# Four stacked layers on one core: the steps of the windowed attention put into another order on every engine

## The chip, the cores and the metric

The kernel runs on one core of a Trainium2 chip. The metric is device time in microseconds (us) for one execution of the whole kernel; a median of several runs is given. A core has five engines that each work through their own instructions in order and wait for one another by semaphores: TensorE (PE, matmuls and transposes, results into PSUM), VectorE (DVE), ScalarE (ACT), GpSimd (POOL) and SyncE (SP), which here only issues DMAs.

## The reference: what is computed

The input has 8 images of 128 channels and 56 x 56 pixels. Four layers follow one another, each as x = x + layer(group norm(x)): a windowed attention (layer 0), a recurrent network over the pixels (layer 1), a partly masked 3x3 convolution (layer 2) and a residual pair of 3x3 convolutions (layer 3). The change touches layer 0 alone, which is in the main:

```python
proj = xw @ W_qkv + b_qkv                   # 49 windows of 8x8 pixels per image
logit = einsum('npc,nqc->npq', q_win * SCALE, k_win)     # window means
r_idx = top_k(logit, 4)                                  # 4 windows for each window
k_sel, v_sel = kv of those 4 windows                     # 256 keys
attn = softmax(einsum('bmqc,bmkc->bmqk', q_h * SCALE, k_sel))   # 8 heads of 16 channels
o = einsum('bmqk,bmkc->bmqc', attn, v_sel)
out = (o + depthwise3x3(v_img)) @ W_o + b_o
```

## The kernel before, in words

All is in fp32. Layer 0 has 8 x 49 = 392 windows, worked off as 196 pairs. One loop iteration p (L739 to L803) does the softmax of pair p+1 and finishes pair p. Its steps are:

- `scores(p+1)` (L492, matmul L504): 8 matmuls for the two windows of the pair, into four PSUM banks `s0` to `s3`, one buffer each. Bank g holds heads of group g for both windows, so a bank is free for the next pair when both exponentials that read it are done.
- `maxima` (L510, L512, DVE): one reduction per bank, four in all. `exponentials` (L514, L517, ACT): eight per pair, one per window and bank, each needs the maximum of its bank.
- `turn(W)` (L534, L540, PE): eight transposes of a window's exponentials into the PSUM tiles `pt0` and `pt1` (one buffer each), then two copies to SBUF, `pt0` by DVE (L542) and `pt1` by ACT (L543). The first window E of pair p+1 is turned at the end of iteration p, the second window O of pair p in the middle of iteration p.
- `divisors` (L522): a reciprocal on DVE (`rden`, L525) and two products on POOL (`rc`, L528); `turn_divisors` (L545, L549): two transposes on PE into the tile `po`.
- `values(p)` (L551, L559): 16 matmuls into `po`; they need both windows' copies and the fetched values `vs`. `spread` (L564, ACT) and `divide` (L568, DVE) read `po`.
- `gather` (L467, POOL) copies the chosen keys for pair p+2 (8 copies, 2 products). `fetch` (L482, SP) issues 8 DMAs per pair for the chosen values, with 6 window buffers.
- small pieces, one matmul group and one evacuation each, all through one PSUM bank `pp` (pool `ps_p`): queries (L380, evacuated L384 on DVE), keys (L283, L292 DVE), value image (L296, L302 ACT), value pixels (L314, L326 DVE), projection (L436, L441 DVE, and a `bn_stats` L449 that is put into `tails`), depthwise convolution (24 matmuls L410, evacuated L417 on ACT).
- "light" pieces of the next images: mean (L211, then 4 tiny DVE operations), variance (L224, 3 tiny DVE operations, then a Newton iteration of 12 tiny operations on POOL, L246 to L249), window means (L339) and routing (L350, then 4 tiny DVE operations).

The order on PE, ACT, DVE and POOL is written out by hand (`tc.manual_schedule`, L621): each engine runs its instructions in the order in which the loop body issues them. A planner (L697 to L714) decides ahead which small pieces go into which pair: `one` and `two` are two small pieces, or `two` is a depthwise convolution and there is usually no `one`; a `light` piece may come on top. In this text a **short pair** has two small pieces and a **long pair** has a depthwise convolution. In the loop of the kernel before, the piece `one` is issued ahead of `turn(O)`, its evacuation behind the copies of O, and the light piece at the very end behind `divide`. Before the loop there is a preamble for image 0 (L630 to L655); in it the PSUM tiles of the pieces go round the six banks of the scores and `pt`, and after it (`begun`) they all go to `pp`.

In the order of the issue in the old loop, a short pair is:

```python
PE :  scores  one  turn(O)  turn_divisors  values  two  turn(E)  light
DVE:  max0 max1  copy0(O)  end of one  max2 max3  hooks  end of two  tails  rden  copy0(E)  divide  light
ACT:  exp00 exp01  copy1(O)  exp10 exp11 exp02 exp03 exp12 exp13  spread  end of two (image)  copy1(E)
```

(expOG is window O, bank G; "hooks" are normalisations L270 with sums L275, and statistics L205, of later images.)

Of the kernel before, what the change touches and what calls it, by code (L numbers as in the profile page):

```python
# [44 lines left out]
def conv_stack_kernel(ctx: ExitStack, tc: tile.TileContext, a: dict, out: bass.AP):  # L45
# [80 lines left out]
    with ExitStack() as l0:  # L126
# [57 lines left out]

        def psum(shape, name):

            pool, tag = (ps_p, "pp") if begun else next(banks)
            return pool.tile(shape, F32, name=name, tag=tag)

        def store(wait, engine, dst, src):  # L190
# [320 lines left out]
            s_ = pairs[p]  # L511
            nc.vector.tensor_reduce(s_["nmax"][:, g, :], s_["s"][g], AX.X, ALU.max, negate=True)  # L512

        def exponentials(p, o, gs):  # L514
            s_ = pairs[p]
            for g in gs:
                nc.scalar.activation(  # L517
                    wins[2 * p + o]["e"][:, g, :], s_["s"][g][:, o, :], AF.Exp, bias=s_["nmax"][:, g, o : o + 1],
                    accum_out=s_["den"][:, o, g : g + 1],
                )  # L520

        def divisors(p):  # L522

# [10 lines left out]
        def turn(W):  # L534

            s_ = wins[W]
            pt = [ps_t.tile([P, 4, P], F32, name=f"pt_{W}_{c}", tag=f"pt{c}") for c in range(2)]
            for c in range(2):
                for g in range(4):
                    nc.tensor.transpose(pt[c][:, g, :], s_["e"][:, g, c * P : (c + 1) * P], ident)  # L540
            s_["eT"] = [win.tile([P, 4, P], F32, name=f"eT_{W}_{c}", tag=f"eT{c}") for c in range(2)]
            nc.vector.tensor_copy(s_["eT"][0], pt[0])  # L542
            nc.scalar.copy(s_["eT"][1], pt[1])  # L543

        def turn_divisors(p):  # L545

            po = pairs[p]["po"] = ps_o.tile([P, 2, 2, 2 * WPX], F32, name=f"po_{p}", tag="po")
            for o in range(2):
                nc.tensor.transpose(po[:, o, 1], pairs[p]["r"][:, o].rearrange("p g c -> p (g c)"), ident)  # L549

        def values(p):  # L551

            po = pairs[p]["po"]
            for o in range(2):
                s_ = wins[2 * p + o]
                for c in (1, 0):
                    for g in range(4):
                        ch = slice(g * CL, (g + 1) * CL)
                        nc.tensor.matmul(  # L559
                            po[ch, o, 0], s_["vw"][:, c, ch], s_["eT"][c][:, g, :],  # L560
                            start=(c == 1), stop=(c == 0),
                        )
# [25 lines left out]
        def run(f):  # L588
            for part in f[:2]:
                part()  # L590

# [50 lines left out]
        for i in (1, 3, 5):  # L642
            normalise(i, True)
        for f, i in ((normalise, 0), (normalise, 2), (sums, 0), (sums, 1), (normalise, 4), (sums, 2), (sums, 3),
                     (normalise, 6), (sums, 4), (sums, 5), (sums, 6)):
            f(i)
        for i in range(NBLK):
            run(keys[i])
# [1 line left out]
        pixels[0][0]()  # L650
        run(route)
        pixels[0][1]()
        for f in (queries(0, 0), image[0], image[1], *pixels[1:-1]):
            run(f)
        nc.scalar.activation(root, eps, AF.Exp)  # L655
        begun.append(True)
        job(-1, -1, lambda: pixels[-1])
        hook(-1, lambda: tails.extend(lambda f=f: run(f) for f in (queries(0, 1), image[2], image[3])))
        for i in range(4, NBLK):
            job(-1, min(pair_of(0, (i - 2) * NW) + 1, 2 * i), lambda i=i: image[i], True)  # L660
        hook(-1, lambda: neighbours(0, 0))

# [6 lines left out]
                job(last + 2, last + 5, lambda b=b, i=i: project(b, i))  # L669
        for b in range(1, B):  # L670

            at = [FIRST + (i > 2) for i in range(NBLK)] if b == 1 else [pair_of(b - 2, 0) + i for i in range(NBLK)]
            if b > 1:
                for i in range(NBLK):
                    hook(max(at[i] - 8, FIRST + i // 2), lambda b=b, i=i: load_x(b, i, i + 1, nc.gpsimd))
            for i in range(NBLK):
# [23 lines left out]
        for p in range(FIRST, END + 6):  # L700
            ready = [t for t in jobs if t[1] <= p and all(placed.get(k, p) < p for k in t[7])]
            light, long = (next((t for t in ready if t[5] == k), None) for k in (LIGHT, LONG))
            ready = [t for t in ready if t[5] == ONE]
            one = next((t for t in ready if not t[4]), None)
            if long:
                one, two = one if len(ready) > MANY else None, long
            else:
                two = next((t for t in ready if t is not one), None)
            plan[p] = (one, two, light)
            for t in filter(None, plan[p]):  # L710
                assert p <= t[0], ("late", p, t)
                jobs.remove(t)
                placed[t[6]] = p
# [25 lines left out]
        for p in range(FIRST, END + 6):  # L739
            now, then = 0 <= p < END, 0 <= p + 1 < END  # L740
            long = plan[p][1] and plan[p][1][5]
            one, two, light = (t and t[3]() for t in plan[p])
            E, O = 2 * p + 2, 2 * p + 1
            if then:
                scores(p + 1)
            if p + 2 < END:
                gather(E + 2)
                gather(E + 3)
                if p > FIRST + 1:
                    fetch(E + 2)  # L750
                    fetch(E + 3)
            for f in later:
                f()
            later.clear()
            for W in (2 * p - 2, 2 * p - 1):
                b, w = divmod(W, NWIN)
                if 0 <= b < B and w % NW == NW - 1:
                    join(b, w // NW)
            if then:
                maxima(p + 1, 0)  # L760
                maxima(p + 1, 1)
                exponentials(p + 1, 0, (0, 1))
            if one:
                one[0]()
            if now:
                turn(O)
                turn_divisors(p)
            if one:
                one[1]()
            if then:  # L770
                maxima(p + 1, 2)
                maxima(p + 1, 3)
                exponentials(p + 1, 1, (0, 1))
                exponentials(p + 1, 0, (2, 3))
                exponentials(p + 1, 1, (2, 3))
            early = two and (not one or long == LONG)
            if early:
                two[0]()
            if now:
                values(p)  # L780
                spread(p)
            if p == END - 1:
                nc.scalar.activation(root, eps, AF.Sqrt)
            if two and not early:
                two[0]()
            for f in hooks.get(p, ()):
                f()
            if two:
                two[1]()
            for f in tails:  # L790
                f()
            tails.clear()
            if then:
                divisors(p + 1)
                turn(E)
            if now:
                divide(p)
            if light:
                light[0]()
                light[1]()  # L800
            if p == FIRST + 1:
                for W in range(4):
                    fetch(W)  # L803
        for f in later:
            f()
        later.clear()
# [816 lines left out]
```

## Time and profile before

| what | value |
|---|---|
| median of 3 runs (lowest to highest) | 3633.07 us (3633.0 to 3638.25) |
| the profiled execution | 3636.9 us, its span 3635.1 us |
| layer 0 in the profile | about 0 to 1365 us |
| first and last score block (pair 0, pair 195) start | 27.71 us, 1358.17 us |
| layer 0, 0 to 1365 us: busy PE, DVE, ACT, POOL | 1306.96, 1098.33, 1093.96, 921.78 us |
| the other layers, 1365 to 3635.1 us: busy PE | 2241.41 of 2270.10 us |
| mean granted TensorE clock | 0.993 |

How to read it: an engine's busy time is the union of its instructions' times. PE's is modelled, so PE at 96% says that something was always in its pipeline, not that it ran at its rate. What paces layer 0 is therefore read from the start of one pair's score block to the start of the next, called a pair's period here. The starts of the score matmuls (L504) give 195 periods with a mean of 6.82 us and a median of 6.61 us. From pair 50 to pair 148 (four images) 98 periods take 666.8 us: 58 short pairs without a light piece take 6.58 us each (6.39 to 7.17), 24 long pairs without one 6.97 us (6.61 to 7.59), 8 short pairs with a light piece behind a DVE-evacuated piece 6.65 us, 4 short pairs with a light piece behind an image piece 8.32 us, and 4 long pairs with a light piece 7.86 us.

### The profile page before, as it was taken

How to read it: one execution, taken by the hardware profiler on the slowest of the kernel's cores; microseconds unless marked ns; L12 is line 12 of the kernel's file. 1: busy time of each engine (PE TensorE's matmuls, PEld its weight loads, DVE VectorE, ACT ScalarE, POOL GpSimd, SP SyncE). 2: the span in 40 equal slices, each digit the busy share in tenths (PEclk: the TensorE clock that was granted, in tenths of full speed). 3: DMA queues.
4: the chain of work that ended last, by engine and by line, in shares of the span. 5: the costliest groups of instructions: out<-in, count | busy, mean ns of one | idle time of the engine just before them, and what ended most of it. 6: DMA issues, size and time to landing. Idle time of an engine off the chain costs nothing.

```text
span 3635.1 us, 88662 instructions
## 1 busy us (share of the span) xinstructions
PE 3548.4 (98%) x31368; PEld 2936.7 (81%) x31368; DVE 1878.2 (52%) x3949; ACT 1673.0 (46%) x5263; POOL 1368.3 (38%) x3734
## 2 busy tenths in 40 slices
PE   8999999999999999999999999999999999999998
PEld 5666666666666668999999999999999833899998
DVE  6888888888888773222111111111122356757665
ACT  5787888888888883222222222222211245122222
POOL 4767677776666661111111111111000156323221
PEclk8999999999999999999999999999999999999999
DMA  5444444444444431111000000000022266000000
GB/s 146 120 121 115 111 123 112 124 113 122 108 107 111 121 91 56 47 44 47 1 1 1 1 1 1 1 1 1 7 57 59 55 171 170 21 21 26 29 21 35
DMA packets 201122, 238.25 MB, mean 66 GB/s; under 512 B 43120, under 2 KB 157680, under 8 KB 200672
## 3 DMA queue, kind: packets, MB, share of 16 engines
q0 software_dynamic: 34624, 117.03, 12.2%
q1 hardware_dynamic: 165216, 115.12, 11.4%
q8 instruction: 254, 4.16, 0.5%
q14 instruction: 196, 1.61, 0.2%
q10 hardware_dynamic: 832, 0.33, 0.0%
HBM read 133.80 MB, written 67.56 MB: 55 GB/s over the span
## 4 chain that ended last, share of the span: by engine, by line
PE 86%; DVE 6%; ACT 5%; issue 3%; POOL 0%; DMA 0%; SPq 0%; POOLq 0%; DVEq 0%; ACTq 0%
PE ps L950 32%; PE pt L540 8%; PE pc3b L1327 7%; PE pc3a L1327 7%; PE s L504 5%; PE po L985 5%; PE po L559 4%; PE pc L1173 4%; PE plep L410 3%; ACT e L517 3%; PE pi L925 2%; DVE nmax L512 2%; PE pc L1181 1%; PE pq L380 1%; PE pk L283 1%
## 5 line engine op out<-in xcount | busy, mean ns | idle before, releaser
L950 PE MATMUL ps<-hs,w_gates 128*128 128x136 f32 x7680 | 932.9, 280 | 0.4 <-DVE gk L962 0.4
L950 PEld LDWEIGHTS ps<-hs,w_gates 128*128 128x128 f32 x7680 | 911.1, 190 | 8.6 <-issue 0.6
L517 ACT ACTIVATE e<-s,nmax 128x256 f32<-128x256 f32 x1568 | 730.9, 479 | 245.2 <-DVE nmax L512 241.4
L973 ACT ACTIVATE hs<-ps,bg 128x136 f32<-128x136 f32 x744 | 237.3, 370 | 933.6 <-PE ps L950 926.1
L928 DVE SCALAR_TENSOR_TENSOR inp<-pi,bine,th 128x272 f32<-128x272 f32 x186 | 84.8, 497 | 888.7 <-ACT th L927 888.7
L512 DVE TENSOR_REDUCE nmax<-s 128x2 f32<-128x512 f32 x784 | 501.9, 682 | 22.5 <-PE s L504 22.3
L540 PEld LDWEIGHTS pt<-ident,e 128*128 128x128 f32 x3136 | 354.3, 141 | 187.0 <-issue 104.3
L540 PE MATMUL pt<-ident,e 128*128 128x128 f32 x3136 | 449.6, 279 | 26.1 <-ACT e L517 7.5
L914 POOL TENSOR_TENSOR xn<-X,ctr 128x136 f32<-128x136 f32 (+1 forms) x186 | 96.3, 537 | 874.9 <-PE pi L925 871.1
L950 PEld LDWEIGHTS ps<-inp,w_gates 128*128 128x128 f32 x2976 | 370.2, 190 | 13.5 <-PE pi L925 1.1
L950 PE MATMUL ps<-inp,w_gates 128*128 128x136 f32 x2976 | 375.3, 279 | 0.7 <-DVE inp L928 0.7
L517 ACT ACTIVATION_READ_ACCUMULATOR e<-s,nmax 128x1 f32 x1568 | 323.3, 206 | 0.0
L474 POOL COPY ks<-kT 128x64 f32 x1568 | 298.2, 234 | 48.3 <-ACT vrow L302 23.6
L528 POOL TENSOR_TENSOR rc<-rden,own 128x128 f32<-128x128 f32 x392 | 147.7, 396 | 372.1 <-DVE rden L525 236.2
L542 DVE COPY eT<-pt 128x512 f32<-128x512 f32 x392 | 263.6, 672 | 24.7 <-PE pt L540 16.8
L1327 PE MATMUL pc3b<-vb,u_w2c_t 128*128 128x224 f32 x1344 | 257.6, 353 | 0.0
L1327 PE MATMUL pc3a<-va,u_w1c_t 128*128 128x224 f32 x1344 | 255.6, 353 | 1.5 <-DVE va L1317 1.5
L1327 PEld LDWEIGHTS pc3a<-va,u_w1c_t 128*128 128x128 f32 x1344 | 254.2, 190 | 1.5 <-POOL va L1316 1.5
L1327 PEld LDWEIGHTS pc3b<-vb,u_w2c_t 128*128 128x128 f32 x1344 | 253.6, 190 | 0.0
L504 PE MATMUL s<-ks,qm 32*128 32x256 f32 x3136 | 250.1, 402 | 0.2
L543 ACT COPY eT<-pt 128x512 f32<-128x512 f32 x392 | 235.6, 601 | 5.4 <-PE pt L540 4.1
L559 PE MATMUL po<-eT,vs 128*32 128x128 f32 x6272 | 226.6, 277 | 10.6 <-ACT eT L543 10.5
(232 smaller groups left out, 4472.2 us busy)
## 6 DMA issues: line engine op xcount, KB each, us to landing
vs<-vpix SPq DMA_DIRECT2D x1568, 32.0 KB
v<-vimg POOLq DMA_DIRECT2D x56, 290.0 KB, 4.0
v<-vimg POOLq DMA_DIRECT2D x56, 289.5 KB, 4.9
v<-vimg POOLq DMA_DIRECT2D x56, 289.0 KB, 5.8
kept<-gk SPq DMA_DIRECT2D x56, 272.0 KB
g<-kept SPq DMA_DIRECT2D x56, 272.0 KB
xkeep<-X POOLq DMA_DIRECT2D x56, 224.0 KB, 2.4
out_dram<-y SPq DMA_DIRECT2D x56, 224.0 KB
```

The source lines that it names most:

```text
L474: nc.gpsimd.tensor_copy(kw[:, t : t + 1, :], ks[b][:, bass.ds(at, 1), :])
L504: nc.tensor.matmul(s_["s"][g][:, o, :], w["qm"][h].rearrange("p h x -> p (h x)"), w["kw"][h], start=True, stop=True,)
L512: nc.vector.tensor_reduce(s_["nmax"][:, g, :], s_["s"][g], AX.X, ALU.max, negate=True)
L517: nc.scalar.activation(wins[2 * p + o]["e"][:, g, :], s_["s"][g][:, o, :], AF.Exp, bias=s_["nmax"][:, g, o : o + 1], accum_out=s_["den"][: ...
L540: nc.tensor.transpose(pt[c][:, g, :], s_["e"][:, g, c * P : (c + 1) * P], ident)
L542: nc.vector.tensor_copy(s_["eT"][0], pt[0])
L543: nc.scalar.copy(s_["eT"][1], pt[1])
L559: nc.tensor.matmul(po[ch, o, 0], s_["vw"][:, c, ch], s_["eT"][c][:, g, :], start=(c == 1), stop=(c == 0),)
L950: nc.tensor.matmul(ps[f][:, i], w, src, start=(i == 0 and k == 0 and h != fresh), stop=(k == KH - 1 if h else k == KI - 1 and (s < WARM or ...
L973: nc.scalar.activation(hs[f][:, s % 2, i], ps[f][:, i], AF.Tanh, bias=bg[:, m : m + 1])
L985: nc.tensor.matmul(po, wout[:, k, :], hs[k // 2][:, :, k % 2], start=(k == 0), stop=(k == KH - 1))
L1327: nc.tensor.matmul(m[k], u[:, dy, k, :], v[:, k, i * WS + dy : i * WS + dy + WS, :], start=(dy == 0), stop=(dy == 2),)
```

## The change

The loop body becomes two written-out orders of named steps, one for long pairs (and for pairs with a scalar piece alone) and one for the rest. The second window is turned right behind the scores; in short pairs the piece `one` stands between that and `turn_divisors`/`values`, and its evacuation `end1` goes behind the third maximum. In long pairs all four maxima run before copy 0 of the second window, the first window's exponentials run first, and `turn_divisors` goes behind `values`. In both, ACT copies the turned first window (`new1`) ahead of the evacuation `end2`; DVE copies it (`new0`) ahead of `tails`, and `light`, `divisors` and `divide` come last, in this order. So on POOL a variance's Newton iteration now stands ahead of `rc`.

The planner no longer puts a light piece into a pair whose `two` is evacuated by ACT, unless it is due. The statistics of image 1 go into the preamble, except three; the seventh pixels piece goes into the preamble too; value-image block 2 uses the bank of `po` for once, and block 3 becomes a planned piece.

```diff
-            pool, tag = (ps_p, "pp") if begun else next(banks)
+            pool, tag = begun[-1] if begun else next(banks)
...
-            nc.vector.tensor_copy(s_["eT"][0], pt[0])
-            nc.scalar.copy(s_["eT"][1], pt[1])
+        def turned(W, c):
+            s_ = wins[W]
+            (nc.scalar.copy if c else nc.vector.tensor_copy)(s_["eT"][c], s_["pt"][c])
...
         for f, i in ((normalise, 0), (normalise, 2), (sums, 0), (sums, 1), (normalise, 4), (sums, 2), (sums, 3),
-                     (normalise, 6), (sums, 4), (sums, 5), (sums, 6)):
+                     (normalise, 6), (sums, 4), (sums, 5), (sums, 6), (once(measure, 1)[0], 0),
+                     (once(measure, 1)[0], 1)):
...
-        for f in (queries(0, 0), image[0], image[1], *pixels[1:-1]):
+        run(queries(0, 0))
+        for i in range(2, 4):
+            once(measure, 1)[0](i)
+        for f in (image[0], image[1], *pixels[1:]):
             run(f)
         nc.scalar.activation(root, eps, AF.Exp)
-        begun.append(True)
-        job(-1, -1, lambda: pixels[-1])
-        hook(-1, lambda: tails.extend(lambda f=f: run(f) for f in (queries(0, 1), image[2], image[3])))
-        for i in range(4, NBLK):
+        begun.append((ps_p, "pp"))
+
+        def second():
+
+            run(queries(0, 1))
+            begun.append((ps_o, "po"))
+            image[2][0]()
+            begun.pop()
+            image[2][1]()
+
+        hook(-1, lambda: tails.append(second))
+        for i in range(3, NBLK):
...
+            if light and two and two[4] and p < light[0]:
+                light = None
...
-            if then:
-                maxima(p + 1, 0)
-                maxima(p + 1, 1)
-                exponentials(p + 1, 0, (0, 1))
-            if one:
-                one[0]()
-            if now:
-                turn(O)
-                turn_divisors(p)
-            if one:
-                one[1]()
...
-            if then:
-                divisors(p + 1)
-                turn(E)
-            if now:
-                divide(p)
-            if light:
-                light[0]()
-                light[1]()
...
+        SHORT = """scores gather turn1 max0 max1 one turned old0 max2 exp00 exp01 old1 exp10 values end1 exp11 max3
+            two exp02 exp03 exp12 exp13 hooks turn0 spread new1 end2 new0 tails light divisors divide"""
+        LONGER = """scores gather turn1 max0 max1 exp00 old1 one end1 max2 max3 exp01 two old0 values turned exp02
+            exp03 exp10 exp11 exp12 exp13 hooks turn0 spread new1 end2 new0 tails light divisors divide"""
...
+            for name in (LONGER if plan[p][1] and (not plan[p][0] or plan[p][1][5] == LONG) else SHORT).split():
+                if name in acts:
+                    acts[name]()
```

In these strings `turn1`, `old0` and `old1` are the transposes and the two copies of the second window O, `turn0`, `new0` and `new1` those of the first window E; `turned` is `turn_divisors`, `end1` and `end2` are the evacuations of `one` and `two`. `gather` holds the gathers, the fetches, the stores put off from earlier pairs and the joins, as before.

More of the change, by code (lines that the diff above doesn't have):

```diff
@@ L512, in maxima, with exponentials @@
             nc.vector.tensor_reduce(s_["nmax"][:, g, :], s_["s"][g], AX.X, ALU.max, negate=True)
-        def exponentials(p, o, gs):
+        def exponentials(p, o, g):
             s_ = pairs[p]
[L516 to L520, printed above, removed]
+            nc.scalar.activation(
+                wins[2 * p + o]["e"][:, g, :], s_["s"][g][:, o, :], AF.Exp, bias=s_["nmax"][:, g, o : o + 1],
+                accum_out=s_["den"][:, o, g : g + 1],
+            )
         def divisors(p):
@@ L536, in turn, with outcome @@
             s_ = wins[W]
-            pt = [ps_t.tile([P, 4, P], F32, name=f"pt_{W}_{c}", tag=f"pt{c}") for c in range(2)]
+            s_["pt"] = [ps_t.tile([P, 4, P], F32, name=f"pt_{W}_{c}", tag=f"pt{c}") for c in range(2)]
             for c in range(2):
                 for g in range(4):
-                    nc.tensor.transpose(pt[c][:, g, :], s_["e"][:, g, c * P : (c + 1) * P], ident)
+                    nc.tensor.transpose(s_["pt"][c][:, g, :], s_["e"][:, g, c * P : (c + 1) * P], ident)
             s_["eT"] = [win.tile([P, 4, P], F32, name=f"eT_{W}_{c}", tag=f"eT{c}") for c in range(2)]
-            nc.vector.tensor_copy(s_["eT"][0], pt[0])
-            nc.scalar.copy(s_["eT"][1], pt[1])
+        def turned(W, c):
+            s_ = wins[W]
+            (nc.scalar.copy if c else nc.vector.tensor_copy)(s_["eT"][c], s_["pt"][c])
+        def outcome(p):
+            if "po" not in pairs[p]:
+                pairs[p]["po"] = ps_o.tile([P, 2, 2, 2 * WPX], F32, name=f"po_{p}", tag="po")
+            return pairs[p]["po"]
         def turn_divisors(p):
-            po = pairs[p]["po"] = ps_o.tile([P, 2, 2, 2 * WPX], F32, name=f"po_{p}", tag="po")
+            po = outcome(p)
             for o in range(2):
@@ L551, in values @@
         def values(p):
-            po = pairs[p]["po"]
+            po = outcome(p)
             for o in range(2):
@@ L670, in conv_stack_kernel @@
         for b in range(1, B):
-            at = [FIRST + (i > 2) for i in range(NBLK)] if b == 1 else [pair_of(b - 2, 0) + i for i in range(NBLK)]
+            at = [FIRST + 1] * NBLK if b == 1 else [pair_of(b - 2, 0) + i for i in range(NBLK)]
             if b > 1:
@@ L675, in conv_stack_kernel @@
                     hook(max(at[i] - 8, FIRST + i // 2), lambda b=b, i=i: load_x(b, i, i + 1, nc.gpsimd))
-            for i in range(NBLK):
+            for i in range(4 * (b == 1), NBLK):
                 hook(at[i], lambda b=b, i=i: once(measure, b)[0](i))
@@ L737, in conv_stack_kernel, with ahead @@
             cut += n
[L739 to L743, printed above, removed]
-            if then:
-                scores(p + 1)
-            if p + 2 < END:
[L747 to L751, printed above, removed]
+        SHORT = """scores gather turn1 max0 max1 one turned old0 max2 exp00 exp01 old1 exp10 values end1 exp11 max3
+            two exp02 exp03 exp12 exp13 hooks turn0 spread new1 end2 new0 tails light divisors divide"""
+        LONGER = """scores gather turn1 max0 max1 exp00 old1 one end1 max2 max3 exp01 two old0 values turned exp02
+            exp03 exp10 exp11 exp12 exp13 hooks turn0 spread new1 end2 new0 tails light divisors divide"""
+        def ahead(p):
+            if p + 2 < END:
+                for W in (2 * p + 4, 2 * p + 5):
+                    gather(W)
+                for W in (2 * p + 4, 2 * p + 5) if p > FIRST + 1 else ():
+                    fetch(W)
             for f in later:
@@ L758, in conv_stack_kernel @@
                     join(b, w // NW)
-            if then:
-                maxima(p + 1, 0)
-                maxima(p + 1, 1)
-                exponentials(p + 1, 0, (0, 1))
-            if one:
-                one[0]()
-            if now:
-                turn(O)
-                turn_divisors(p)
-            if one:
-                one[1]()
[L770 to L775, printed above, removed]
@@ L776, in conv_stack_kernel, with every, rest, root_table @@
-            early = two and (not one or long == LONG)
-            if early:
-                two[0]()
-            if now:
-                values(p)
-                spread(p)
+        def every(fs):
+            for f in fs:
+                f()
+        def rest():
+            every(tails)
+            tails.clear()
+        def root_table(p):
             if p == END - 1:
                 nc.scalar.activation(root, eps, AF.Sqrt)
-            if two and not early:
-                two[0]()
@@ L786, in conv_stack_kernel @@
-            for f in hooks.get(p, ()):
-                f()
-            if two:
[L789 to L793, printed above, removed]
-                divisors(p + 1)
-                turn(E)
-            if now:
-                divide(p)
-            if light:
-                light[0]()
-                light[1]()
-            if p == FIRST + 1:
-                for W in range(4):
-                    fetch(W)
+        for p in range(FIRST, END + 6):
+            now, then = 0 <= p < END, 0 <= p + 1 < END
+            one, two, light = (t and t[3]() for t in plan[p])
+            E, O = 2 * p + 2, 2 * p + 1
+            acts = {
+                "gather": lambda: ahead(p), "hooks": lambda: every(hooks.get(p, ())), "tails": rest,
+            }
+            if then:
+                acts.update(scores=lambda: scores(p + 1), divisors=lambda: divisors(p + 1), turn0=lambda: turn(E),
+                            new0=lambda: turned(E, 0), new1=lambda: turned(E, 1))
+                for g in range(4):
+                    acts[f"max{g}"] = lambda g=g: maxima(p + 1, g)
+                    for o in range(2):
+                        acts[f"exp{o}{g}"] = lambda o=o, g=g: exponentials(p + 1, o, g)
+            if now:
+                acts.update(turn1=lambda: turn(O), old0=lambda: turned(O, 0), old1=lambda: turned(O, 1),
+                            turned=lambda: turn_divisors(p), values=lambda: values(p), divide=lambda: divide(p),
+                            spread=lambda: (spread(p), root_table(p)))
+            if one:
+                acts.update(one=one[0], end1=one[1])
+            if two:
+                acts.update(two=two[0], end2=two[1])
+            if light:
+                acts["light"] = lambda: run(light)
+            for name in (LONGER if plan[p][1] and (not plan[p][0] or plan[p][1][5] == LONG) else SHORT).split():
+                if name in acts:
+                    acts[name]()
+            for W in range(4) if p == FIRST + 1 else ():
+                fetch(W)
```

## The prediction

> **What bounds the kernel now.** I read busy time by stretches first, then the chain of work that ended last, then each engine's timeline over one short pair. Layer 0 repeats almost exactly from image to image, so one pair says much.
>
> Busy time over 200 to 1200 us (columns: length, then PE, PE weight load, DVE, ACT, POOL, granted clock, DMA share, GB/s):
>
> ```profile
> 200.00:1200.00 1000.00, 968.61 (x11445) 657.91 (x11443) 827.50 (x1617) 817.82 (x2885) 698.33 (x2201) 1.00 0.45 114
> ```
>
> No engine but PE is full, and PE's number is modelled. The chain over two short pairs (start, length, what):
>
> ```profile
> 618.28 0.23 PE pt L540 x2
> 618.52 0.18 ACT e L517
> 618.70 0.04 issue
> 618.75 0.77 PE pt L540 x5
> 619.51 1.27 PE s L504 x16
> ...
> 624.06 0.95 PE pk L283 x2
> 625.01 0.23 PE pt L540 x2
> 625.25 0.19 ACT e L517
> ```
>
> PE is in it nearly always, but at each pair's end turn(E) stops for an exponential: PE is early there, and the softmax is what is late. DVE shows why:
>
> ```profile
> 620.71 1.28 DVE L512 TENSOR_REDUCE nmax<-s 128x2 f32<-128x512 f32 x2
> 622.34 0.69 DVE L542 COPY eT<-pt 128x512 f32<-128x512 f32 x1 [0.35 <-PE pt L540]
> 622.95 0.68 DVE L326 TENSOR_TENSOR vp<-pvp,bv_row 128x512 f32<-128x512 f32 x1
> 623.55 1.28 DVE L512 TENSOR_REDUCE nmax<-s 128x2 f32<-128x512 f32 x2
> ```
>
> Its copy of window O waits 0.35 us, because PE runs the piece `one` (1.00 us here) before turn(O); then the end of `one` stands ahead of the third maximum. ACT starts exp03 at 624.86, as the fourth maximum ends (624.83).
>
> So a short pair's loop is: max0 at t; exp03 at t+4.15 (620.71 to 624.86); 0.48 to its end (625.34); 0.84 from there through five transposes to the next scores (626.18); 1.27 from those to max0 (619.44 to 620.71; 1.17 where the scores don't wait). Sum 6.74 us, which is this period (619.44 to 626.18).
>
> **PE's own floor**, from starts of successive groups when nothing waits: scores 1.08, transposes 0.87 twice, `po` L549 0.31, values 1.10, pieces 0.86 (pixels 1.00): 5.95 us for a short pair. With a depthwise convolution (2.28) in place of two pieces 6.4; the trace has 6.61, and 6.80 when the scores wait 0.19 for the last exponential. Long pairs are PE's, short pairs the softmax's.
>
> **The change, part by part.**
>
> *turn(O) behind the scores; max2 ahead of end1 (short pairs).* No instruction is added. DVE issues these operations 0.60 us apart: max0 t, max1 t+0.60, copy t+1.21 (its transposes are then 0.5 us old, so the 0.35 wait goes), max2 t+1.81, end1 t+2.41, max3 t+3.01, done t+3.69. On ACT, from rows of pair 613 and this one: exp00 t+0.79, exp01 t+1.32, copy t+1.84, exp10 t+2.32, then 0.46 each: exp03 t+3.70. Maximum and ACT meet; I take t+3.73. The loop is 3.73+0.47+0.84+1.27 = 6.31, or 6.2 after a long pair. What is late next: everything nearly at once. PE's `two` needs the bank `pp`, so end1 (t+3.09), plus about 0.09: at t+3.18, then 0.86 and 0.87 and 0.1 to the scores, t+5.01, against t+5.04 for the exponential chain. With pixels as `two` PE is later by 0.1. I take 6.33 for short pairs on short pairs and 6.19 after long ones.
>
> *DVE's end of the pair.* The old order is rden, copy(E), divide after the last exponential, so max0 came right behind divide (gap -0.08 us in most pairs). Now only rden and divide (0.15+0.42) follow it. Without hooks max0 is free at 7.23 and due at 7.57: hidden. With `tails` (0.57 of DVE pitch) it is 0.23 late; with normalisation, sums and statistics together plus tails 0.8 to 0.95 late, of which a following long pair, PE's by 0.4, hides half. Counted over the planned pairs: 2.9 us in two images. The old wait for turn(O) absorbed such delays; that cover is gone.
>
> *Long pairs.* Same PE work in another order: 6.75, as before; exp13 ends at 6.3. The long pairs at 7.26 to 7.59 started with max0 at about 2 to 2.25 us, behind hooks; that falls by about half.
>
> *Lights.* In long pairs and behind images PE waited for ACT to free `pp`: 7.86 against 6.80, 8.32 against 6.58. Those waits go (four images: 4x1.06 + 4x1.74 = 11.2 us). But a light now stands ahead of rden, `rc` and divide. Mean 0.5, window means 0.55, routing 0.8 us (0.31 of PE, and 0.6 to 1.0 of DVE against the slack of 0.34). The variance is worst, on POOL:
>
> ```profile
> 605.67 0.76 POOL L528 TENSOR_TENSOR rc<-rden,own 128x128 f32<-128x128 f32 x2 [0.87 <-DVE rden L525]
> 607.16 0.19 POOL L246 TENSOR_TENSOR nr<-r 128x1 f32<-128x1 f32 x1 [0.74 <-DVE r L242]
> ...
> 610.16 0.19 POOL L249 TENSOR_TENSOR r<-r,nr 128x1 f32<-128x1 f32 x1
> ```
>
> Twelve operations take 3.2 us, 4.2 from the matmul's start. With `rc` behind them its second half ends at about 11.3 us from the pair's start; the next pair's `po` transposes stand ahead of `values` on PE and want it at 9.5: 1.5 us of stall, 0.4 more with tails, plus 0.31. Queued behind `rc` on POOL are the gathers (2.2 us), done by 13.8, just before the delayed scores. About 2.0 us each. All lights: 3.85 us per image, against some 3.6 now: a wash.
>
> *end2 behind new1 on ACT.* spread 0.38, new1 0.60, image 0.70 from 6.4: ends at 8.05, and the next pair's exp00 is due at 8.35, its `one` at 8.44. Hidden by 0.3; if not, up to 0.3 in 49 pairs.
>
> *SP.* Its instructions are not moved, but the pair gets shorter. Fetches over the same 1000 us:
>
> ```profile
> L487 SPq DMA_DIRECT2D vs<-vpix x1179: 468/469/1726, 199.9 to 1199.9; - x197
> ```
>
> At best one window takes 3.03 us (four transfers 0.65 apart, one load of indices), a pair 6.05; long issues (durations over 0.47 sum to 74 us in layer 0) and pauses make 6.50 per pair. Values are fetched about 12 us ahead. My mean below is 6.63, so SP follows, just. It caps the gain at about 60 us.
>
> *Start.* Three statistics (1.67 us) leave the path ahead of the first maximum for DVE's gaps in the preamble (1.3 and 1.2 us); the pixels piece adds 0.25 to the scores' way; block 2 in `po` need not wait for block 3's evacuation. Followed through at the durations below, the second score block starts at 41.0 instead of 44.47: 3.4 us.
>
> ```profile
> 31.47 1.86 PE L380 MATMUL pq<-xw,wqkv 128*128 128x448 f32 x2 [1.46 <-DVE vp L332]
> ```
>
> ```profile
> 30.00:35.00 5.00, 1.87 (x3) 0.50 (x2) 4.97 (x11) 3.86 (x16) 4.21 (x12) 0.63 0.90 276
> ```
>
> Here a rule and a row part. The Trainium skill (TensorE: Matmul & The Clock Gate, "What's actually happening") says that the array goes to half clock after about one idle window of 3.4 us. With the scores followed at once by a piece no such gap need occur: four matmul pairs would take about 0.95 instead of 1.86, and the start would gain 7 us. The row shows half clock at a gap of 1.46 us, in a PE that was busy 1.87 of 5 us. I take the row: 3.4; the rule's 7 is the other bound.
>
> **Sum**, over the 98 pairs of four images that take 666.8 us now: 28 long at 6.75 = 189.0; 28 short after long at 6.19 = 173.3; 42 short at 6.33 = 265.9; DVE delays 5.8; lights 15.4; together 649.4. That is 0.178 us per pair; on the first 170 pairs 30 us; the last 25, with fewer pieces (6.49 on average), 0.1 each, 2.5; the start 3.4. In all 36 us. From the profiled execution's 3636.9 (span 3635.1 and 1.8 around it) to 3600.9; the runs' median lies 3.8 lower: 3597.
>
> **Rivals.**
>
> 1. *More is won*: DVE's idle time absorbs the delays, the variances cost nothing, the start stays at full clock. Then SP sets the pace: 6.50 x 195 = 1268 against 1330, 62 us: 3571. For it: DVE is busy 83%. Against: its order is fixed, and delays to max0 have no slack left. Chance 0.14.
> 2. *The old loop was not the bound in short pairs* (the change does nothing there): one bank `pp` and PE's order hold the period, `two` waiting for end1 that now stands behind max2. If the DVE-to-PE hop costs 0.35 instead of 0.09, the loop is 6.57, as now. Then start and long pairs alone count: 3.4 and some 5: 3625. Its milder half (hop 0.2, gain about 20) belongs to the forecast's range. Chance 0.2, half of it within 7 us of before.
> 3. *Slower*: `rc`. In ordinary short pairs rden now waits behind copy, and `rc` behind POOL's gathers, stores and, every 3.5 pairs, a join of 2.3 us. `rc` ends at 7.7 to 8.3, wanted at 9.3. Each microsecond beyond that stalls `values` in PE's order one for one. From 9.6 in all 125 short pairs the gain is gone; at 9.75 the 0.45 us x 125 = 56 us give 3653. For it: POOL is busy 698 of 1000 us, in order. Against: a margin of 1 us. Chance 0.08.
>
> **Chances.** Forecast (gain 15 to 52) 0.58; the others as above. 0.2%, some 7 us, is about what a measurement of this kernel can tell from no change. Faster: 0.58+0.14+0.10 = 0.82; same 0.10; slower 0.08. The forecast's own range is 3581 to 3618. To leave out no more than 2 in 10 it reaches towards rival 1 and into rival 2: 3568 to 3629.
>
> **What would show it.** Right: short-pair periods of 6.2 to 6.4; the wait of DVE's copy for L540 gone from short pairs; exp03 at 3.7 us after max0; long pairs at 6.75; pairs after a variance about 8 us with PE waiting for POOL's `rc`; second score block at 41 us. Wrong: short pairs at 6.55 with PE's piece waiting for DVE; SP issuing back to back with PE waiting for `vs`; PE waiting for `rc` in ordinary pairs.

## The result, and the profile after

| what | before | after |
|---|---|---|
| median of 4 runs (lowest to highest) | 3633.03 us (3631.27 to 3638.25) | 3603.55 us (3601.88 to 3605.56) |
| ratio, 95% interval | | 0.9917, 0.99 to 0.9934 |
| the profiled execution, its span | 3636.9 us, 3635.1 us | 3601.88 us, 3599.6 us |
| first, second, last score block start | 27.71, 44.47, 1358.17 us | 28.08, 37.07, 1329.15 us |
| from the last score block to the end of the span | 2276.9 us | 2270.4 us |
| mean granted TensorE clock | 0.993 | 0.996 |

The kernel is 29.5 us faster by the medians, against a forecast of 36 (3597 us, with a range of 3581 to 3618). In the profiled executions layer 0 is 29.0 us shorter (1358.17 to 1329.15). In all they differ by more, 35 us, because the untouched rest also ran 6.5 us shorter in the one that was profiled after. That part is the execution's, not the change's, and the agreement of 3601.88 with the 3600.9 that the prediction's sum gives is partly luck.

Busy time over 200 to 1200 us after (length, PE, PE weight load, DVE, ACT, POOL, clock, DMA share, GB/s):

```profile
200.00:1200.00 1000.00, 966.24 (x11675) 666.57 (x11674) 830.69 (x1648) 823.65 (x2951) 712.34 (x2252) 1.00 0.46 118
```

PE is a little less busy than before, though it does 2% more work in the same time (x11675 against x11445): so it now waits somewhere. DVE in a short pair after, which answers to its timeline of before (the pair starts at 665.10):

```profile
666.26 1.29 DVE L512 TENSOR_REDUCE nmax<-s 128x2 f32<-128x512 f32 x2 [0.40 <-PE s L504]
667.47 0.68 DVE L544 COPY eT<-pt 128x512 f32<-128x512 f32 x1
668.06 0.68 DVE L512 TENSOR_REDUCE nmax<-s 128x2 f32<-128x512 f32 x1
668.66 0.67 DVE L384 TENSOR_SCALAR q<-pq,bqkv 128x448 f32<-128x448 f32 x1
669.25 0.68 DVE L512 TENSOR_REDUCE nmax<-s 128x2 f32<-128x512 f32 x1
```

The copy's wait for the transposes (0.35 us before) is gone, the maximum comes ahead of the piece's end, and max0 starts 1.16 us after the scores, waiting for them and for nothing else. The period is 6.18 us (665.10 to 671.28). exp03 starts 3.7 us after max0.

What is late instead is in the waits over 200 to 1200 us (engine and line, what it waited for: us in total, times, longest):

```profile
PEld po L556 <- POOL rc L527: 12.6, 16, 2.1
PE po L566 <- DMA vs<-vpix: 12.3, 16, 1.4
...
PE po L556 <- POOL rc L527: 8.3, 5, 1.8
```

`rc` was foreseen: five variances, where `turn_divisors` waits. The second row, `values` waiting for the fetched values, is new: before, PE's matmuls had no such row. The weight load of the same work overlaps, so rows of PE and PEld are not added. And one fetch wait is larger than all others. In what follows, the number of a single pair is that of its loop iteration p: its period runs from the start of score block p+1 to that of p+2. The chain of work around pair 174 (start, length, what):

```profile
1194.76 1.15 PE s L504 x16
...
1198.13 4.35 DMA vs<-vpix
1202.48 0.14 issue
1202.62 0.41 PE po L566 x5
```

SP's timeline over the same stretch shows what stood between the fetches:

```profile
1179.76 3.50 SPq L487 DMA_DIRECT2D vs<-vpix  x5
1183.36 0.63 SPq L744 DMA_DIRECT2D w_gates<-in_w_hh_t_dram  x1
1184.60 6.53 SPq L487 DMA_DIRECT2D vs<-vpix  x8
1191.19 0.58 SPq L745 DMA_DIRECT2D w_gates<-in_w_ih_t_dram  x1
```

Two weight loads for layer 1 (1024 and 512 KB) stand in SP's queue between the fetches. That pair took 11.97 us, with a transfer of values that landed 4.35 us after its issue. The same loads cost nothing before (6.40 us): values were then issued 14.0 us ahead of their use in the median and never less than 7.1, against 7.0 and 1.7 now (end of a window's last issue to its first use, over layer 0). In the text below this time is called the lead.

### The profile page after: what moved, and what is told of

The parts are those of the page before. It is cut to its first block, busy times and chain, and to the rows that moved or that the text cites. A ratio compares the mean times of both kernels' runs of the same rounds, so it can differ in the third digit from the quotient of the medians.

```text
span 3599.6 us, 88461 instructions
## 1 busy us (share of the span) xinstructions
PE 3508.2 (97%) x31368; PEld 2927.0 (81%) x31368; DVE 1864.1 (52%) x3949; ACT 1657.1 (46%) x5263; POOL 1364.8 (38%) x3734
## 3 DMA queue, kind: packets, MB, share of 16 engines
q0 software_dynamic: 34624, 117.03, 12.3%
q8 instruction: 253, 4.15, 0.5%
## 4 chain that ended last, share of the span: by engine, by line
PE 83%; DVE 6%; issue 3%; ACT 3%; DMA 3%; SPq 1%; POOL 1%; POOLq 0%; DVEq 0%; ACTq 0%
PE ps L968 32%; PE pc3b L1345 7%; PE pc3a L1345 7%; PE pt L539 7%; PE po L1003 5%; PE s L504 5%; PE pc L1191 4%; PE plep L410 4%; PE po L566 3%; PE pi L943 2%; DMA vs<-vpix 2%; DVE nmax L512 2%; ACT e L516 2%; PE pc L1199 1%; PE pvt L296 1%
## 5 line engine op out<-in xcount | busy, mean ns | idle before, releaser
L539 PE MATMUL pt<-ident,e 128*128 128x128 f32 x3136 | 430.3, 279 | 6.1 <-ACT e L516 4.4
L968 PEld LDWEIGHTS ps<-inp,w_gates 128*128 128x128 f32 x2976 | 370.2, 190 | 13.5 <-PE pi L943 1.1
L516 ACT ACTIVATION_READ_ACCUMULATOR e<-s,nmax 128x1 f32 x1568 | 331.7, 212 | 0.0
L566 PEld LDWEIGHTS po<-eT,vs 128*32 128x32 f32 x6272 | 159.2, 109 | 106.7 <-issue 48.2
```

Source lines behind the costliest of these rows:

```text
L516: nc.scalar.activation(wins[2 * p + o]["e"][:, g, :], s_["s"][g][:, o, :], AF.Exp, bias=s_["nmax"][:, g, o : o + 1], accum_out=s_["den"][: ...
L539: nc.tensor.transpose(s_["pt"][c][:, g, :], s_["e"][:, g, c * P : (c + 1) * P], ident)
L566: nc.tensor.matmul(po[ch, o, 0], s_["vw"][:, c, ch], s_["eT"][c][:, g, :], start=(c == 1), stop=(c == 0),)
L968: nc.tensor.matmul(ps[f][:, i], w, src, start=(i == 0 and k == 0 and h != fresh), stop=(k == KH - 1 if h else k == KI - 1 and (s < WARM or ...
```

## The experiments

The theory under test: the new order does shorten the short pair's loop, by the place of turn(O) above all; but SP's queue, which the prediction took to follow just behind, becomes the pace of layer 0, so that whatever is won beyond it turns into waits for values. The rivals: `rc` or the lights hold the time; the bank `pp` does; the gain is the start's. No kernel leaves any work out. Layer 0's columns come from the score starts of each profiled execution: "last block" is the start of pair 195's, "four images" the 98 periods of the prediction's sum. From the last score block to the end, which no kernel changes, the profiled executions differ by up to 13.5 us, so times are compared by the medians and by their ratios to the kernel before, which was run beside each of them (its median lay between 3630.82 and 3633.21 us). What layer 0 shows is from one execution each.

| kernel | median, us | ratio, 95% interval | four images | last block |
|---|---|---|---|---|
| before | 3633.03 | 1 | 666.8 | 1358.2 |
| after | 3603.55 | 0.9917 (0.99 to 0.9934) | 650.1 | 1329.2 |
| old_turn_early | 3618.68 | 0.9964 (0.9951 to 0.9978) | 656.7 | 1342.0 |
| one_first | 3641.7 | 1.0026 (1.002 to 1.0033) | 670.7 | 1358.8 |
| end1_first | 3604.28 | 0.9925 (0.9911 to 0.9938) | 648.7 | 1319.0 |
| first_start | 3598.39 | 0.9893 (0.9878 to 0.9909) | 645.4 | 1325.9 |
| old_rule | 3638.13 | 1.0015 (1.0008 to 1.0021) | 672.2 | 1361.6 |
| light_last | 3600.96 | 0.9908 (0.9894 to 0.9921) | 642.7 | 1319.6 |
| quarter_fetch | 3603.22 | 0.9918 (0.9905 to 0.9931) | 654.5 | 1326.3 |
| light_last_quarter | 3609.45 | 0.9929 (0.9917 to 0.9941) | 660.6 | 1332.5 |
| old_quarter_fetch | 3658.47 | 1.0071 (1.0058 to 1.0084) | 679.1 | 1380.8 |
| pair_load | 3585.4 | 0.9869 (0.9854 to 0.9884) | 642.5 | 1310.8 |
| light_last_pair_load | 3585.21 | 0.9871 (0.9856 to 0.9886) | 642.0 | 1310.4 |
| old_pair_load | 3632.1 | 1.0002 (0.9994 to 1.001) | 667.0 | 1357.0 |

**Is SP's queue the pace?** Two ways of taking work off it. In quarter_fetch (and old_quarter_fetch, the same in the kernel before), POOL issues the last of each window's four transfers, in `gather`:

```diff
+                if W >= 4 and t == TOPK - 1:
+                    nc.gpsimd.dma_start(vw[WPX:, 1, :], vpix[b % 2][bass.ds(at, 1)].rearrange("o x c -> (o x) c"))
```

> The changed kernel with the fourth of the four value transfers of each window issued by POOL inside gather (from window 4 on) instead of by SP. Theory 2 (SP's 6.6 us per pair is the bound now): SP's share falls from some 6.6 to 5.0 us per pair, the lead of the fetches goes back to 11 us or more, PE no longer waits for values (about 2.5 us per image): 3580 to 3588 us. Rival (the late landings come from DMA load, not from SP's queue, or POOL's two further DMAs of 0.57 us per pair delay rc and the gathers): 3600 us or slower, with PE waiting for POOL's rc.

> The kernel before with the same quarter of the fetches on POOL. Theory 2 says that there SP reached the limit of its 6 buffers again and again and PE hardly waited for values: no gain, 3630 to 3636 us. If SP had been a bound in the kernel before already: 3615 us or less.

The fetch waits went (short pairs with one: 70 from 7.26 to 6.19 us, 98 from 7.42 to 6.18), but the time stayed. POOL's issue takes 0.55 to 0.6 us of an in-order engine, and the waits over 200 to 1200 us in quarter_fetch say who is late now:

```profile
PEld po L568 <- POOL rc L539: 28.9, 57, 4.0
...
PE po L568 <- POOL rc L539: 12.2, 8, 3.3
```

57 waits for `rc` against 16. In the kernel before, with SP not late, nothing was there to win and 25 us were lost; PE's scores wait for POOL's gathers there (3.9 us over 200 to 1200 us, a wait of which before has none), which explains a part. So this pair of runs shows POOL's small margin (the prediction's third rival is true of a POOL with 1.1 us more work per pair), and doesn't decide on SP. The second way costs no engine anything: in pair_load SP loads the indices of both windows of a pair at once, one register load instead of two.

```diff
+            n = 2 if W % NWIN + 1 < NWIN else 1
+            idx = chosen(W, mybir.EngineType.SP, n)
+            for i in range(2):
+                fetch_one(W + i, idx[i * TOPK : (i + 1) * TOPK] if i < n else chosen(W + i, mybir.EngineType.SP))
...
-            for t, at in enumerate(chosen(W, mybir.EngineType.SP)):
+            for t, at in enumerate(idx):
```

> The changed kernel in which SP loads the indices of both windows of a pair with one instruction (8 values) instead of two (4 each), where both are of one image; the 8 transfers stay on SP. Theory 2 (SP's queue is the bound between images' slow places; PE waits for values that were issued too late): SP needs some 0.35 us less per pair, 6.25 instead of 6.6, the lead of the fetches grows by 2 to 4 us, the waits for values (about 10 us in four images, 20 in all) go for the most part: 3586 to 3594 us. Rival (the waits come from slow landings whatever the lead): 3600 us or more.

> The kernel before with the same paired index load. By theory 2 SP had no more to give there than its 6 buffers allow: no change, 3630 to 3636 us. If the fetch queue was already a bound: 3620 us or less.

This decides. The changed kernel gains another 18.2 us by the medians (17 by the ratios, 18.4 in layer 0 of the profiled executions); the kernel before gains nothing, its interval holding 1. The same saving is worth 17 to 18 us in one order and nothing in the other, so the queue is a bound after and was none before. The saving itself is smaller than the 0.35 us per pair that was expected: a load of eight indices takes 0.52 us in the median, one of four 0.30, and an undisturbed pair of fetches goes from 6.05 to 5.92 us. SP's issues over 1000 us, after and in pair_load (count, duration min/median/max in ns):

```profile
L487 SPq DMA_DIRECT2D vs<-vpix x1203: 468/469/1907, 200.0 to 1199.9; - x172
```

```profile
L496 SPq DMA_DIRECT2D vs<-vpix x1219: 468/469/2037, 200.1 to 1199.5; - x175
```

At 8 per pair these are 6.65 and 6.56 us per pair. After, the window buffer that a fetch writes had been free for at least 4.5 us when its first transfer was issued (9.6 in the median): SP never waited for a buffer, it issued back to back. Before, the smallest such margin was 0.06 us (median 3.15 over layer 0), and in pair_load it is 0.06 again (median 5.5): there SP catches up with its buffers now and then, though the queue is still close to the pace. PE's matmul waits for values over 200 to 1200 us fall from 12.3 us to this row of pair_load:

```profile
PE po L575 <- DMA vs<-vpix: 0.6, 1, 0.6
```

Nothing of this says that the queue has one fixed rate. In light_last, below, SP issues the same fetches and never waits for a buffer either (margin at least 4.1 us), yet it takes 6.60 us per pair over 200 to 1200 us and not 6.65: its long DMA instructions take 65 us above 0.47 each over layer 0, against 72. Why, no run shows.

**Is it the lights?** light_last puts `divisors` ahead of `light` in both orders, so that `rc` doesn't wait for a Newton iteration.

```diff
-            two exp02 exp03 exp12 exp13 hooks turn0 spread new1 end2 new0 tails light divisors divide"""
+            two exp02 exp03 exp12 exp13 hooks turn0 spread new1 end2 new0 tails divisors light divide"""
```

> The changed kernel with divisors issued ahead of light in both orders, so that rc stands ahead of the variance's Newton operations on POOL. Theory 1 (the Newton operations hold rc, and rc holds values on PE): the pairs behind a variance fall from 7.8 to 8.3 us to about 6.3, five or six of them with about 1.8 us each: 3594 us. Theory 2 (SP's queue of fetches sets the pace, and PE's stall there only lets SP catch up): the stall goes, but PE waits for values instead a few pairs on, gain at most 3 us: 3600 to 3603 us.

> Both edits of the changed kernel together (divisors ahead of light, a quarter of the fetches on POOL). If SP's queue hides what is saved at the variances, the two together give more than the sum of each alone: 3570 to 3576 us. If they are independent: the sum of the two single gains.

> The same with divisors ahead of light. With SP out of the way, the variance's stall that was taken away shows in full (about 7.5 us in four images, from the pairs behind a variance, some 9 in all): 3576 to 3585 us by theory 2; by the rival the same as with divisors ahead of light alone, about 3601 us.

The pairs behind a variance do fall (60: 7.80 to 6.18 us; 84: 8.32 to 6.53), and the wait of PE's weight loads for `rc` goes from 16 waits of 12.6 us to 8 of 1.7. Part comes back one pair later, where POOL's gathers, and in 85 a join, are late instead (61: 6.61 to 6.91; 85: 6.19 to 7.88); over the four variances of the four images 4.5 us are left. Layer 0 of the profiled execution is 9.6 us shorter, but the median falls by 2.6 us only, less than the intervals can tell. On top of pair_load the same pairs gain 4.3 us and the whole nothing (0.9871 against 0.9869): PE waits 2.8 us for values instead of 0.6 over 200 to 1200 us, pair 77 goes from 6.64 to 9.45 us, and SP again never waits for a buffer. On top of quarter_fetch there is no gain either (3609.45 against 3603.22, the intervals overlapping). So the lights are a real term, of about 1 us per variance net, but no run turns it into a gain that the medians can tell, and with pair_load it comes back as waits for values.

**What of the order is it?** old_turn_early puts turn(O) ahead of `one` in the kernel before, nothing else; one_first takes just that back in the changed kernel's short pairs; end1_first takes the other swap back, on DVE. The three edits, in this order:

```diff
+            if now:
+                turn(O)
             if one:
                 one[0]()
             if now:
-                turn(O)
                 turn_divisors(p)
...
-        SHORT = """scores gather turn1 max0 max1 one turned old0 max2 exp00 exp01 old1 exp10 values end1 exp11 max3
+        SHORT = """scores gather one turn1 max0 max1 turned old0 max2 exp00 exp01 old1 exp10 values end1 exp11 max3
...
-        SHORT = """scores gather turn1 max0 max1 one turned old0 max2 exp00 exp01 old1 exp10 values end1 exp11 max3
+        SHORT = """scores gather turn1 max0 max1 one turned old0 end1 max2 exp00 exp01 old1 exp10 values exp11 max3
```

> The kernel before with one edit: turn(O) is issued right behind the scores, ahead of the piece one; the order on DVE, ACT and POOL stays, the planner and the preamble too. My theory (in short pairs DVE's copy waited for these transposes and held the third and fourth maximum): max0 to the end of max3 falls from 3.9 to 4.1 us to 3.7, short pairs from 6.58 to 6.2 to 6.35, that is 25 to 35 us: 3598 to 3608 us. Rival (the gain of the whole change comes from max2 ahead of end1, from the long pairs, lights and the start): 3625 us or more.

> The changed kernel, only that in short pairs PE issues the piece ahead of the transposes of the second window, as the kernel before did; all else stays in the changed order. Theory (the place of the transposes is what shortens the short pair, because DVE's copy stands between the second and the third maximum and waits for them): short pairs without a light piece go from 6.18 to 6.45 to 6.55 us at their base, the wait of the copy for the transposes comes back at about 0.35 us, four images take 663 to 668 us, in all 3622 to 3632 us. Rival (the new end of DVE's pair and the third maximum ahead of the piece's evacuation are what counts, as the turn alone gave only 15 us in the kernel before): the base stays under 6.3 us and the whole at 3603 to 3615 us.

> The changed kernel, only that in short pairs DVE evacuates the piece ahead of the third maximum, as before. Theory (maxima and exponentials are the loop, DVE's operations follow one another 0.60 us apart): the third maximum comes 0.6 us later, but the fourth ends at the same place, so the exponentials, which meet the maxima there, lose little: base of short pairs 6.2 to 6.35 us, in all 3603 to 3613 us. Rival (the bank of the small pieces is the bound, since the second piece waits for the first one's evacuation): the second piece starts 0.6 us earlier and the base falls to 5.9 to 6.1 us, in all 3585 to 3600 us.

Alone, the early turn is worth 13 us by the ratio, half of what was expected (16 in layer 0 of the profiled executions). Taken away from the changed kernel, it costs 40 us by the ratios (30 in layer 0): at least the whole gain, and more than was expected. Short pairs without a light then mostly take 6.59 to 7.15 us instead of 6.18, and DVE's copy waits again. DVE in one_first:

```profile
684.82 1.29 DVE L512 TENSOR_REDUCE nmax<-s 128x2 f32<-128x512 f32 x2 [0.40 <-PE s L504]
686.48 0.69 DVE L544 COPY eT<-pt 128x512 f32<-128x512 f32 x1 [0.38 <-PE pt L539]
687.09 0.68 DVE L512 TENSOR_REDUCE nmax<-s 128x2 f32<-128x512 f32 x1
```

The wait is about as long as it was in the old order (0.35), and the fourth maximum ends 4.14 us after max0 starts, as it did there (4.12), against 3.67 after. In the kernel before, the early turn left most short pairs at 6.26 to 6.53 us: copy(E), rden and divide still follow the last exponential there, and in most short pairs that follow a short pair max0 starts only 1.27 to 1.40 us after the scores (mostly 1.16 after). The gains of the single edits do not add up to that of the change. end1_first takes the same time as after. Its short pairs are dearer by 0.08 to 0.35 us (55: 6.27, 53: 6.53, 52: 6.59), a little more than was expected, but the lead is 11.2 us in the median there against 7.0, and PE's matmuls no longer wait for values over 200 to 1200 us. (Layer 0 of its profiled execution is 10 us shorter, 7.5 of them in the last 25 pairs; the median shows nothing of that.) DVE evacuated the first piece 0.5 us earlier there, yet the second piece on PE started 4.15 us after the scores against 4.29 in the changed kernel. So `pp` came free earlier and the second piece hardly moved: the bank isn't the bound.

**The planner's rule and the start.** old_rule is the kernel before with the new rule for lights alone (the two lines with `light = None` in the change); first_start is the changed kernel with the preamble of before (the hunks on `sums`, `queries(0, 0)`, `second` and the hooks of image 1 taken back).

> The kernel before with the planner's new rule alone (no light piece into a pair whose second piece is evacuated by ACT, unless it is due). Theory (the lights in long pairs and behind image pieces cost 1.06 and 1.74 us each, four of each in four images, and cost next to nothing elsewhere): 8 to 16 us are won over layer 0, 3617 to 3625 us. Rival (what the rule takes from these pairs comes back in the pairs that get the pieces, or the pieces fall due later all at once): within 4 us of the kernel before, 3628 to 3635 us.

> The changed kernel with the preamble of the kernel before: all statistics of image 1 ahead of the first maximum, six pixels pieces, value-image blocks 2 and 3 in the tails; the loop stays changed. Theory (TensorE stays at full clock in the new start, so the start is worth the 7.4 us that stand between the second score blocks): second score block back at about 44.5 us, the loop as in the changed kernel, about 3611 us. Rival (the start is worth the 3.4 us of the prediction, and the rest of the 7.4 us is given back later, to fetched values that come no earlier): second score block at 44.5 us all the same, but about 3607 us or less.

The rule takes the dear pairs away (57: 8.31 to 6.94 us; 65: 7.92 to 6.81), 9.7 us in four images. But the variances that it sends into short pairs make the pair after them dear: 61 goes from 6.81 to 10.95 us, 85 from 6.59 to 8.96, with two more like them 12.5 us. The Newton iteration on POOL in old_rule:

```profile
456.82 0.20 POOL L246 TENSOR_TENSOR nr<-r 128x1 f32<-128x1 f32 x1 [0.60 <-DVE r L242]
...
460.32 0.77 POOL L474 COPY ks<-kT 128x64 f32 x4 [0.29 <-issue]
```

The gathers for the next scores, and behind them a join and `rc`, start only when it is over. The rule alone is slower by 0.15%, where 8 to 16 us had been expected as its gain.

In first_start the rival holds, and goes further than it was put: the second score block came at 42.8 us (44.5 expected), and the whole is, if anything, faster than with the new start (0.9893 against 0.9917; the intervals overlap). By how much each profiled execution leads the kernel before, at one score block:

| block | after | first_start | pair_load |
|---|---|---|---|
| 1 | 7.4 us | 1.6 us | 7.5 us |
| 100 | 23.1 | 21.7 | 29.4 |
| 195 | 29.0 | 32.3 | 47.4 |

The 5.8 us that the new start is ahead have shrunk to 1.4 by block 100 and are gone by the end. The first fetch is issued at 34.45 us before, 35.16 after and 36.33 in first_start, whatever the scores do, so a start that lets PE begin earlier shortens the lead of the values: the first pair's are 3.3 us ahead of their use after, 7.7 in first_start, 10.7 before.

## Why the prediction came out so

Layer 0's gain by the prediction's terms (blocks by the score starts; the 98 pairs split by kind, a short pair's base being 6.185):

| term | predicted, us | measured, us |
|---|---|---|
| start, to the second block | 3.4 | 7.4 |
| blocks 1 to 170 | 30 | 26.6 |
| last 25 pairs | 2.5 | -5.0 |
| layer 0 | 36 | 29.0 |
| of the 98 pairs: 28 long | 189.0 | 189.4 |
| 70 short, base | 439.2 | 433.0 |
| DVE delays | 5.8 | 1.7 |
| lights, variances included | 15.4 | 16.3 |
| waits for values (8 short pairs) | 0 | 9.7 |
| together | 649.4 | 650.1 |

*Short pairs.* The mechanism was right, and turn(O) is its core (one_first). The term mis-sized is the 1.27 from the scores to max0 in short pairs on short pairs: 1.16 was measured in most of them, as after long pairs, so 6.19 holds in both and not only after long pairs. 42 pairs at 0.14 us make nearly the 6.2 us between the two sums.

*DVE's end of the pair.* Put too high: hooks and tails did delay max0, but only 1.7 us are left over in four images, outside pairs with a light or a fetch wait.

*Long pairs* as foreseen: 6.76 on average against 6.75. The floor of 6.4 that the prediction gives PE in them is a slip: its own terms make 6.51 (5.95 less two pieces of 0.86, plus 2.28), nearer to the 6.61 of the traces before and after.

*Lights.* As foreseen in sum and in the variance's mechanism: pairs 60 and 109 take 7.80 us, 84 8.32, 133 10.0, PE waiting for `rc`. old_rule and light_last show that it isn't specific to `rc`: behind `rc` in POOL's order the iteration delays the next pair's gathers instead.

*SP.* This is the step that failed. "My mean below is 6.63, so SP follows, just" set a capacity of 6.50 us per pair against a mean of 6.63. In the changed kernel the queue, which never waits for a buffer there, runs at 6.63 (over layer 0) to 6.65 (200 to 1200 us), and at 6.60 in light_last: 0.10 to 0.15 us more. Of the terms of 6.50, the 6.05 of a pair at best stand, and so do the long issues (0.37 us per pair above 0.47 each after, 0.38 before, 0.33 in light_last); what was too small is the pauses, 0.08 taken and 0.21 left by 6.63. So the lead of the values shrank from 14.0 us to 7.0 in the median, and delays that the lead had covered (slow transfers, the weight loads) reached PE: 9.7 us in four images, some 6 us in pair 174 alone. In the sum it happened to cancel what the short pairs and DVE gave more. The prediction's own sign for a wrong forecast, "SP issuing back to back with PE waiting for `vs`", is what the profile shows, although the total came close.

*Start.* Here the bound by the rule was right and the row was misread. PE in the changed start and in first_start:

```profile
32.08 1.02 PE L296 MATMUL pvt<-xw,wqkv 128*128 128x448 f32 x2 [1.24 <-DVE q L384]
```

```profile
32.12 1.86 PE L380 MATMUL pq<-xw,wqkv 128*128 128x448 f32 x2 [2.06 <-DVE vp L332]
```

The granted clock over 30 to 35 us:

```profile
30.00:35.00 5.00, 2.86 (x12) 1.33 (x12) 4.96 (x10) 4.69 (x18) 4.32 (x14) 1.00 0.92 278
```

```profile
30.00:35.00 5.00, 2.94 (x9) 1.95 (x9) 4.97 (x11) 3.86 (x16) 4.41 (x13) 0.62 0.98 267
```

After a gap of 1.24 us (and one of 1.26 at 35.37) the clock stays at 1.00 and a matmul pair takes 1.02 us; after 2.06 us, as after 1.46 before, it takes 1.86. The Trainium skill (TensorE: Matmul & The Clock Gate, "What's actually happening") puts the drop after about one idle window of 3.4 us. Its conclusion for this start, full clock and 7 us, came true; its length didn't, since half clock followed a gap of 1.46 us before. Whether the gap's length alone decides, these three starts do not show. The prediction carried the half clock over from a start in which PE had a gap to one in which a piece follows the scores at once. But the 7.4 us bought nothing that the runs can tell: first_start, without them, is no slower, so the right value of this term for the total was about nothing.

*The rivals.* The first, SP as the cap, was the nearest to what happened, at 6.63 and not 6.50, and so with half of its 62 us. The second, the bank `pp`, is refuted by end1_first. The third, `rc` in ordinary pairs, didn't come: its waits are the variances'. quarter_fetch, with 1.1 us more of POOL per pair and 57 waits, shows that its margin was about as thin as the 1 us stated.

*What stays open.* Why the new order without the early turn is dearer (670.7 us in four images) than the old order without it (666.8) was not taken apart further. That first_start is faster than after by 0.24% is inside the intervals. The waits of pair 174 are read from the trace; moving the weight loads to another place wasn't tried. The index load taken away doesn't remove all of them: in pair_load pair 174 takes 6.90 us, but pair 179 takes 9.21, of which PE waits 3.0 for values (6.11 after). Why light_last and end1_first, with a layer 0 some 10 us shorter in the profiled execution, are not faster by as much in the medians is not known.

## What to carry to other kernels

When a change speeds a loop up, work out the capacity of every queue that only follows it, from its own issue times at full load, and compare it with the new period: a queue with 2% in hand by a sum of rows may have nothing in hand, and it shows first as a shrinking lead, then as waits in single iterations. A saving is worth what the bound of that order makes of it: one index load less per pair gave some 18 us after the change and nothing before it, and 7 us at the start gave nothing in a kernel whose queue set the pace. Test a reordering both ways, the part alone and the whole without it: here 13 and 40 us for the same swap.

## What the runs showed of the hardware that was not expected

A transfer of 32 KB lands 2.5 us after its issue in the median, but on the chain after twelve took 4.7 to 6.2 us between 200 and 1200 us. One of 6.14 us was issued at 504.04, while three loads of 290 KB, issued by POOL from 502.73 to 504.43, were landing (3.9 to 5.8 us each). A lead of values that looks ample by the median isn't. Taking a quarter of the transfers from SP to POOL was a bad trade: 0.55 to 0.6 us of POOL per transfer, for 0.65 us of SP, cost the kernel before 25 us.
